# Five row blocks of a graph layer from gathered rows, and weights asked for one at a time

## The chip, the cores and the metric

The kernel runs on one core of a Trainium2 chip. The core has a matrix engine (TensorE, PE in the profile, with PEld for its weight loads), a vector engine (VectorE, DVE), a scalar engine (ScalarE, ACT), a general engine (GpSimd, POOL), and DMA queues that SyncE (SP), ACT and POOL issue from. Each engine works through its instructions in the order in which the program gives them. The metric is the time of one execution on the device in microseconds, as the median of several runs. The kernel before takes 1496.76 us, median of 3 runs (1496.23 to 1499.8).

## The reference

There are N = 2708 nodes with D = 256 features, and a matrix adj in which about 0.3% of the entries and the diagonal are nonzero. Two layers follow one another. Layer 0 is the part that the change is in:

```python
support = adj @ x
support = jnp.concatenate([x, support], axis=1)
x = _layernorm(x + relu(support @ weight + bias))
```

Layer 1 takes R = (adj + I), each row divided by its sum, and twice over does Xf = R @ Xf and Xa = A @ Xa, where A is a softmax attention over all nodes of which each row keeps the fewest largest entries that hold 0.9 of its mass. Each step adds Xf @ U1.T + Xa @ U2.T to Z. Two layer norms end it.

## The kernel before, in words

The nodes are cut into NB = 22 row blocks of P = 128 (the last has 20 rows, and is called EDGE). In DRAM adj is kept by blocks: `adj_d[m, :, k, :]` is the transposed 128 x 128 tile of row block m and column block k, and one DMA of a half row block brings 11 such tiles (704 KB). All arithmetic is float32. The order of the work is written out by hand: the program's order on each engine and on each DMA queue is the order on the chip, and semaphores order the engines among each other.

**Start.** adj @ x @ w0[D:] is computed as adj @ y0 with y0 = x @ w0[D:], so y0 comes first: 22 row blocks (line 385), whose copies out of PSUM alternate between ACT (line 388, odd blocks) and DVE (line 390, even ones). SP's queue loads xT in seven pieces (line 194), then adj of block 0. ACT's queue asks for all weights ahead of its first copy: both halves of w0 (line 188), then b0, w1, w3, w2, the four matrices u1 and u2, and the two rows gb (lines 198 to 206). y0 has one more column of ones, so that the row sums of adj come out of the same product.

**Layer 0's loop** runs over the row blocks m in their order, 0 to 21. In each:

- `name_columns(m)` on DVE finds for each of the 128 partitions which of the 22 tiles holds a nonzero, and writes the name of each such row of adj_d as a number (lines 282 to 288; the diagonal tile is left out). It reads the same halves of adj that PE multiplies.
- `adj_product` on PE multiplies 22 tiles by y0 into a PSUM tile acc, of which there are two (line 250; EDGE has a form of its own at line 247, in four column groups that `edge_sum` adds, and needs its acc zeroed by DVE first).
- SP's queue loads the next block's two halves (line 220). There are three buffers of a half, so the second half waits until PE and DVE have both read the first half of the present block.
- PE adds xT times w0[:D] (line 452), then turns the x1 of the block before (`x1_transpose`, line 430), and after every fourth block `x1_qk` projects queries and keys for 512 columns (lines 415 to 422).
- DVE and ACT do bias, relu, residual and layer norm (lines 461 to 469), and SP stores x1 (lines 467 and 470).

**Lists.** Class `Lists` makes from the names of a group of row blocks the lists of rows to gather. `turn` transposes the names on PE; `take` extracts the eight largest names of each row with a MAX8 and a MATCH_REPLACE8 on DVE (lines 314 and 315), 20 times for a list of 160; `end` packs the pieces through DRAM: a store and a load on POOL's queue (lines 327 and 328), a scan on DVE that waits for them (line 332), seven indirect scatters (line 338), and a load of the list into `ix` (line 341). The groups are blocks 0 to 15, whose list is taken during the last six blocks of layer 0 and ended behind them, and blocks 16 to 21, whose list is made during step 1 of layer 1.

**Layer 1** starts with `begin1` (logits, line 496, and the u1 projections, line 621). It uses the lists: `adj_gather` brings up to 896 rows of adj_d per row block with CC = 7 indirect DMAs of 128 rows on POOL's queue (line 360), so R @ Xf takes 8 products instead of 22. The rows of the other factor are gathered in the same way (line 670). Four large tiles es[0] to es[3] hold the attention rows in layer 1; in layer 0 they hold w0 (es[0]), b0 and w1n (es[1]), and the names and the first list's room (es[3]). The lines that hold the loop's order around a block are

```python
        adj_product(acc, m, y0, D + 1, False)
        if m == EDGE:
            acc = edge_sum(acc, D + 1, False)
        if m + 1 < NB:
            adj_load(m + 1, 0)
            adj_load(m + 1, 1)
```

## Time and profile before

| what | value |
| --- | --- |
| median of 3 runs | 1496.76 us (1496.23 to 1499.8) |
| the profiled execution | 1397.94 us |
| its span, first to last instruction | 1396.1 us |
| mean granted TensorE clock in it | 0.957 |
| PE busy in the span | 1287.6 us (92%) |
| DVE busy | 1054.3 us (76%) |
| ACT busy | 757.1 us (54%) |
| POOL busy | 645.5 us (46%) |
| DMA | 157.95 MB, mean 113 GB/s |

The profile is one execution, and that one was 98.8 us shorter than the median of the runs. Its page gives busy times, the span in 40 slices of 34.9 us each, the groups of instructions by line, and the waits. In a line of the timeline the first number is the start in us, the second the length in us, then come the engine (a q behind it means its queue), the line of the kernel, the operation, what is written and read, the shape, and how many were merged; in brackets stand the idle time before it and what ended that. A float32 matmul shows as two MATMUL instructions. In a line of the windows the columns are the stretch, its length, the busy time of PE, PEld, DVE, ACT and POOL with the number of instructions, the granted clock, the share of the DMA engines' time and GB/s.

### The profile page before, as it was taken

The page shows a single profiled execution, that of the slowest core. Times are in us where ns is not written, and L with a number is a line of the kernel's source. Part 1 is how long each engine was busy: PE and PEld are TensorE (multiplying, and loading weights), DVE is VectorE, ACT ScalarE, POOL GpSimd, SP SyncE. Part 2 cuts the span into 40 slices and gives each one's busy share as a digit, 9 for nine tenths or more (in the row PEclk, how much of TensorE's full clock was granted, in tenths as well). Part 3 has the DMA queues.
Part 4 walks back from the last instruction along what each step waited for, and adds up shares of the span by engine and source line. Part 5 has one row for each costly group of instructions (what it writes and reads, how often), then busy time and mean ns, then how long its engine had stood idle before and what let it go on. Part 6 is the DMA issues. An engine that isn't in the chain of part 4 may idle for free.

```text
span 1396.1 us, 19129 instructions
## 1 busy us (share of the span) xinstructions
PE 1287.6 (92%) x5788; PEld 903.6 (65%) x5788; DVE 1054.3 (76%) x3624; ACT 757.1 (54%) x1381; POOL 645.5 (46%) x595
## 2 busy tenths in 40 slices
PE   5999999989899999999999869999998998999885
PEld 4778778743466666766676447676765665666662
DVE  1445445784988887777771399999999999999995
ACT  1100000015455555555554468887878989998942
POOL 1000000004374431776555287877726557777771
PEclk8999999999999999999999889999999999999986
DMA  7345445422222210232223255464523434544441
GB/s 211 102 147 161 144 157 159 138 83 68 76 74 76 64 62 9 73 93 79 66 65 100 76 162 162 140 182 132 157 62 117 130 117 140 162 138 127 140 129 45
DMA packets 92831, 157.95 MB, mean 113 GB/s; under 512 B 16356, under 2 KB 65196, under 8 KB 92720
## 3 DMA queue, kind: packets, MB, share of 16 engines
q1 hardware_dynamic: 66434, 100.59, 22.2%
q0 software_dynamic: 20544, 51.17, 13.4%
q10 hardware_dynamic: 5742, 4.89, 1.3%
q8 instruction: 48, 0.79, 0.2%
q14 instruction: 63, 0.52, 0.1%
HBM read 125.33 MB, written 31.26 MB: 112 GB/s over the span
## 4 chain that ended last, share of the span: by engine, by line
PE 54%; DVE 38%; ACT 2%; DMA 2%; issue 2%; SPq 0%; ACTq 0%; DVEq 0%
PE acc L536 16%; PE acc L250 15%; PE lg L496 6%; DVE cand L950 6%; DVE w L981 5%; DVE e L984 5%; DVE w L947 4%; PE tr L516 4%; PE misc L649 3%; DVE spare L551 3%; DVE srt L549 3%; PE acc L621 2%; PE misc L420 2%; PE acc L452 2%; PE misc L415 2%
## 5 line engine op out<-in xcount | busy, mean ns | idle before, releaser
L536 PE MATMUL acc<-ya,wT 128*128 128x256 f32 (+1 forms) x924 | 241.2, 402 | 2.8 <-ACT wT L519 2.8
L519 ACT COPY wT<-tr 128x512 f32<-128x512 f32 (+2 forms) x264 | 133.7, 510 | 201.3 <-PE tr L516 198.4
L670 POOL DMA_INDIRECT yg<-yf_d,ix x154 | 196.6, 1276 | 80.6 <-PE misc L702 43.7
L536 PE MATMUL acc<-x,wT 128*128 128x256 f32 (+1 forms) x924 | 230.5, 388 | 0.0
L536 PEld LDWEIGHTS acc<-x,wT 128*128 128x128 f32 (+1 forms) x924 | 165.2, 189 | 79.6 <-issue 46.9
L536 PEld LDWEIGHTS acc<-ya,wT 128*128 128x128 f32 (+1 forms) x924 | 177.8, 199 | 58.0 <-issue 25.7
L250 PE MATMUL acc<-y,adj_t 128*128 128x257 f32 (+1 forms) x924 | 208.8, 382 | 0.0
L670 POOL DMA_INDIRECT yg<-v_d,ix x154 | 169.8, 1103 | 77.6 <-DMA v_d<-v 32.4
L250 PEld LDWEIGHTS acc<-y,adj_t 128*128 128x128 f32 (+1 forms) x924 | 171.5, 189 | 34.0 <-issue 10.3
L360 POOL DMA_INDIRECT adj_t<-in_adj,ix x154 | 169.3, 1099 | 50.9 <-issue 39.6
L496 PE MATMUL lg<-k,q 64*128 64x512 f32 (+3 forms) x528 | 155.3, 617 | 35.3 <-ACT e L794 33.4
L702 PE MATMUL misc<-yg,adj_t 128*128 128x256 f32 (+1 forms) x660 | 175.1, 397 | 12.8 <-DVE v L725 5.2
L516 PE MATMUL tr<-ident,e 128*128 128x128 f32 (+1 forms) x968 | 153.1, 278 | 16.8 <-DVE bulk L985 14.2
L516 PEld LDWEIGHTS tr<-ident,e 128*128 128x128 f32 (+1 forms) x968 | 117.4, 142 | 64.3 <-issue 30.2
L702 PEld LDWEIGHTS misc<-yg,adj_t 128*128 128x128 f32 (+1 forms) x660 | 117.4, 192 | 62.0 <-issue 18.2
L327 POOL DMA_DIRECT2D part_d<-e x1 | 0.6, 573 | 307.5 <-DVE e L326 307.5
L542 DVE MAX8 cand<-e 128x8 f32<-128x170 f32 (+1 forms) x352 | 88.1, 319 | 39.9 <-ACT e L503 39.9
L894 ACT ACTIVATE w<-e,st 128x2708 f32<-128x2708 f32 (+1 forms) x43 | 113.5, 2640 | 0.0
L431 ACT COPY x1T<-tr 128x256 f32<-128x256 f32 (+1 forms) x22 | 8.0, 364 | 192.1 <-PE tr L430 192.1
L897 ACT ACTIVATE w<-e,st 128x2708 f32<-128x2708 f32 (+1 forms) x42 | 111.0, 2642 | 0.1
L950 DVE MAX8 cand<-w 128x8 f32<-128x136 f32 (+1 forms) x440 | 94.4, 285 | 0.8
L549 DVE MAX8 srt<-spare 128x8 f32<-128x128 f32 (+3 forms) x264 | 81.4, 308 | 9.1
(227 smaller groups left out, 1849.4 us busy)
## 6 DMA issues: line engine op xcount, KB each, us to landing
adj_t<-in_adj SPq DMA_DIRECT2D x44, 704.0 KB
adj_t<-adjc_d SPq DMA_DIRECT2D x44, 448.0 KB
adjc_d<-adj_t SPq DMA_DIRECT2D x22, 256.0 KB
base<-za_d SPq DMA_DIRECT2D x41, 128.0 KB
adjc_d<-adj_t SPq DMA_DIRECT2D x22, 192.0 KB
xt<-in_x ACTq DMA_DIRECT2D x21, 128.0 KB
x_d<-x SPq DMA_DIRECT2D x21, 128.0 KB
x1b_d<-xb SPq DMA_DIRECT2D x21, 128.0 KB
```

The lines of the kernel that those rows point to most:

```text
L250: nc.tensor.matmul(acc[:p, :n], lhsT=halves[k // KH][:kw, k % KH, :p], rhs=y[:kw, k, :n], start=k == 0, stop=stop and k == NB - 1)
L360: nc.gpsimd.indirect_dma_start(out=a[:CW, i, :], out_offset=None, in_=adj_rows, in_offset=bass.IndirectOffsetOnAxis(ap=ix[:CW, m, i:i + 1] ...
L496: nc.tensor.matmul(lg[:p, h, :b - a], lhsT=q[o, t * P:t * P + p], rhs=keys[s][o, i, :b - a], start=True, stop=True)
L516: nc.tensor.transpose(tr[:kw, k % 4, :p], e[:p, k * P:k * P + kw], ident[:p, :p])
L519: nc.scalar.copy(wT[:, :full, :p], tr[:, :full, :p])
L536: nc.tensor.matmul(acc[:p, :D], lhsT=wT[:kw, k % 4, :p], rhs=y[:kw, k, :], start=k == 0, stop=k == NB - 1)
L549: nc.vector.max(dst[:p, i:i + 8], src[:p])
L670: nc.gpsimd.indirect_dma_start(out=y[:CW, i, :], out_offset=None, in_=rows_d, in_offset=bass.IndirectOffsetOnAxis(ap=ix[:CW, m, i:i + 1], ...
L702: nc.tensor.matmul(acc[:p, :D], lhsT=a[:kw, k, :p], rhs=rhs, start=k == 0, stop=k == CC)
L894: nc.scalar.activation(scr[:b.p, :N], e, AF.Relu, bias=b.nz, scale=b.l[k], accum_out=b.relu)
L897: nc.scalar.activation(scr[:b.p, :N], e, AF.Sign, bias=b.nz, scale=b.l[k], accum_out=b.sign)
L950: nc.vector.max(cand[:p, 8 * i:8 * i + 8], w[:p, SEG2 * i:SEG2 * (i + 1)])
```

## The change

The row blocks 16 to 20 are no longer multiplied tile by tile in layer 0. Their halves of adj are loaded into free parts of es[0] to es[2] during the first blocks, only to be named (`scan_load`, and a second `name_columns` in the same block); EDGE is brought forward to fourth place, and so the list of the group (16, 22) can be made early: it is turned in the seventh block of the order, taken 7 at a time in three blocks, and ended. y0 is stored to DRAM in the seventh block. Then `gather0` brings the listed rows of adj_d and of y0 with seven indirect DMAs each, and `sparse_product` makes the product from 8 matmuls. The five gathered blocks alternate with the dense blocks 12 to 15 behind block 11; there is room for two at a time. The other two lists are (0, 12), taken during the last blocks, and (12, 16), taken in step 1 of layer 1 where the second list was.

Of the weights, ACT's queue asks for w0[D:] only at first; the others follow one at a time, six between its y0 copies and five in the first blocks of the loop.

```diff
--- before.py
+++ after.py
@@ -37,7 +37,10 @@
 TIE_EPS = 1.5e-5
 KS = 7
 CAP = 160
-ML = 16
+GROUPS = ((16, 22), (0, 12), (12, 16))
+SPARSE = (16, 17, 18, 19, 20)
+
+ORDER = (0, 1, 2, 21, 3, 4, 5, 6, 7, 8, 9, 10, 11, 16, 12, 17, 13, 18, 14, 19, 15, 20)
 CW, CC = 128, 7
 
 
...
@@ -184,9 +189,11 @@
     w0 = es[0][:, :2 * DC * D].rearrange("p (c e) -> p c e", e=D)
     b0 = es[1][:, :D]
     w1n = es[1][:DA, D:2 * D].rearrange("a (c p) -> a c p", p=P)
-    for h in (1, 0):
+    def w0_load(h):
         nc.scalar.dma_start(out=w0[:, h * DC:(h + 1) * DC, :],
                             in_=w0_d[h * D:(h + 1) * D].rearrange("(c p) e -> p c e", p=P))
+
+    w0_load(1)
 
     xT = big.tile([P, DC, N], FP, tag="Y", name="xT")
     xT_v = xT_d.rearrange("(c p) n -> p c n", p=P)
...
@@ -195,15 +202,18 @@
 
     make_identity(nc, ident)
     nc.gpsimd.memset(c.eps, LN_EPS)
-    nc.scalar.dma_start(out=b0, in_=b0_d[None, :].to_broadcast([P, D]))
-    nc.scalar.dma_start(out=c.w1, in_=w1_d.rearrange("(c p) a -> p c a", p=P))
-    nc.scalar.dma_start(out=c.w3, in_=w3_d.rearrange("(c p) a -> p c a", p=P))
-    nc.scalar.dma_start(out=c.w2, in_=w2_d)
-    for s in range(2):
-        nc.scalar.dma_start(out=c.u1[:, :, s, :], in_=u1_d[s].rearrange("(c p) e -> p c e", p=P))
-        nc.scalar.dma_start(out=c.u2[:, :, s, :], in_=u2_d[s].rearrange("(c p) e -> p c e", p=P))
-    nc.scalar.dma_start(out=c.gb[:, 0, :], in_=g_d[None, :].to_broadcast([P, D]))
-    nc.scalar.dma_start(out=c.gb[:, 1, :], in_=b_d[None, :].to_broadcast([P, D]))
+
+    weights = [lambda: w0_load(0),
+               lambda: nc.scalar.dma_start(out=b0, in_=b0_d[None, :].to_broadcast([P, D])),
+               lambda: nc.scalar.dma_start(out=c.w1, in_=w1_d.rearrange("(c p) a -> p c a", p=P)),
+               lambda: nc.scalar.dma_start(out=c.w2, in_=w2_d),
+               lambda: nc.scalar.dma_start(out=c.w3, in_=w3_d.rearrange("(c p) a -> p c a", p=P)),
+               lambda: nc.scalar.dma_start(out=c.gb[:, 1, :], in_=b_d[None, :].to_broadcast([P, D])),
+               lambda: nc.scalar.dma_start(out=c.gb[:, 0, :], in_=g_d[None, :].to_broadcast([P, D]))]
+    for u, u_d in ((c.u1, u1_d), (c.u2, u2_d)):
+        for s in range(2):
+            weights.append(lambda u=u, u_d=u_d, s=s: nc.scalar.dma_start(
+                out=u[:, :, s, :], in_=u_d[s].rearrange("(c p) e -> p c e", p=P)))
     nc.gpsimd.memset(flags, 0.0)
     fcol = small.tile([P, 1], FP, tag="fcol", name="fcol", bufs=1)
     onec = small.tile([P, 1], FP, tag="onec", name="onec", bufs=1)
...
@@ -263,23 +273,23 @@
...
-    def name_columns(m):
+    def name_columns(m, halves):
         for h in range(2):
-            nc.vector.tensor_reduce(some[:, h * KH:(h + 1) * KH], adj_of[m][h], AX.X, ALU.max,
+            nc.vector.tensor_reduce(some[:, h * KH:(h + 1) * KH], halves[h], AX.X, ALU.max,
...
@@ -386,6 +398,8 @@
                              start=j == 0, stop=j == DC - 1)
         if t % 2:
             nc.scalar.copy(y0[:p, t, :D], py[:p, :D])
+            if 3 <= t < 15:
+                weights.pop(0)()
         else:
             nc.vector.tensor_copy(y0[:p, t, :D], py[:p, :D])
 
...
@@ -434,29 +448,108 @@
         a, b = CHS[i]
         qk_project(0, a, b, lambda j: x1T[:, j, a:b])
 
+
+
+
+    scan_room = [r[:, a:a + KH * P].rearrange("p (k i) -> p k i", i=P)
+                 for r, a in ((es[2], 0), (es[0], 2 * DC * D), (es[1], 3 * D))]
+    gather_room = []
+    for (ry, ay), (ra_, aa), ao in (((es[2], 0), (es[0], 2 * DC * D), 0), ((es[1], 3 * D), (es[2], CC * (D + 1)), 1)):
+        ao = 2 * DC * D + CC * P + ao * P
+        gather_room.append((ry[:, ay:ay + CC * (D + 1)].rearrange("p (c d) -> p c d", d=D + 1),
+                            ra_[:, aa:aa + CC * P].rearrange("p (c i) -> p c i", i=P), es[0][:, ao:ao + P]))
+    to_scan, scanned, gathered = list(SPARSE), {}, {}
+    n_scans = 0
+
+    def scan_load():
+        nonlocal n_scans
+        m = to_scan.pop(0)
+        scanned[m] = []
+        for h in range(2):
+            a = scan_room[n_scans % 3]
+            n_scans += 1
+            nc.sync.dma_start(out=a, in_=adj_d[m, :, h * KH:(h + 1) * KH, :])
+            scanned[m].append(a)
+
+    y0_rows = c.y0_d.rearrange("p k d -> (p k) d")
+    to_gather = list(SPARSE)
+
+    def gather0():
+
+        if not to_gather:
+            return
+        m = to_gather.pop(0)
+        y, a, own = gather_room[SPARSE.index(m) % 2]
+        iy = small.tile([P, CC], I32, tag="iy", name="iy", bufs=2)
+        nc.sync.dma_start(out=own, in_=adj_d[m, :, m, :])
+        nc.gpsimd.tensor_scalar(iy[:CW], ix[:CW, m, :], m * P * NB, P * NB - 1, op0=ALU.subtract, op1=ALU.min)
+        for i in range(CC):
+            nc.gpsimd.indirect_dma_start(out=a[:CW, i, :], out_offset=None, in_=adj_rows,
+                                         in_offset=bass.IndirectOffsetOnAxis(ap=ix[:CW, m, i:i + 1], axis=0))
+        for i in range(CC):
+            nc.gpsimd.indirect_dma_start(out=y[:CW, i, :], out_offset=None, in_=y0_rows,
+                                         in_offset=bass.IndirectOffsetOnAxis(ap=iy[:CW, i:i + 1], axis=0))
+        gathered[m] = y, a, own
+
+    def sparse_product(acc, m, y0):
+        y, a, own = gathered.pop(m)
+        for i in range(CC):
+            nc.tensor.matmul(acc[:, :D + 1], lhsT=a[:CW, i, :], rhs=y[:CW, i, :], start=i == 0, stop=False)
+        nc.tensor.matmul(acc[:, :D + 1], lhsT=own, rhs=y0[:, m, :], start=False, stop=False)
+
     CB = CH // P
-    lists = Lists(0, ML, flags[:, NF - 4:NF - 2], first_room)
-    for m in range(NB):
+    TURN = len(SPARSE) + 1
+    dense = [m for m in ORDER if m not in SPARSE]
+    done, n_qk = set(), 0
+
+    def x1_done(m):
+
+        nonlocal n_qk
+        x1_transpose(m)
+        done.add(m)
+        while n_qk < len(CHS) and all(k in done for k in range(CB * n_qk, min(NB, CB * n_qk + CB))):
+            x1_qk(n_qk)
+            n_qk += 1
+
+    lists = Lists(0, first_room)
+    taken = 0
+    scan_load()
+    for i, m in enumerate(ORDER):
         p = rows(m)
         xt = work.tile([P, D], FP, tag="in", name="xt", bufs=3)
         nc.scalar.dma_start(out=xt[:p], in_=x_d[m * P:m * P + p, :])
+        if weights and i:
+            weights.pop(0)()
         acc = edge_acc if m == EDGE else ps_acc()
-        name_columns(m)
-        adj_product(acc, m, y0, D + 1, False)
-        if m == EDGE:
-            acc = edge_sum(acc, D + 1, False)
-        if m + 1 < NB:
-            adj_load(m + 1, 0)
-            adj_load(m + 1, 1)
+        if m in SPARSE:
+            sparse_product(acc, m, y0)
+            gather0()
+        else:
+            name_columns(m, adj_of[m])
+            if scanned and m != EDGE:
+                name_columns(*scanned.popitem())
+            adj_product(acc, m, y0, D + 1, False)
+            if m == EDGE:
+                acc = edge_sum(acc, D + 1, False)
+            dense.pop(0)
+            if dense:
+                adj_load(dense[0], 0)
+                adj_load(dense[0], 1)
+            if to_scan and m != EDGE:
+                scan_load()
+            elif i == len(SPARSE) + 1:
+                for a, b in ((0, KH), (KH, NB - 1)):
+                    nc.sync.dma_start(out=c.y0_d[:, a:b, :], in_=y0[:, a:b, :])
+                nc.sync.dma_start(out=c.y0_d[:rows(NB - 1), NB - 1, :], in_=y0[:rows(NB - 1), NB - 1, :])
         for j in range(DC):
             nc.tensor.matmul(acc[:p, :D], lhsT=xT[:, j, m * P:m * P + p], rhs=w0[:, j, :],
                              start=False, stop=j == DC - 1)
-        if m:
-            x1_transpose(m - 1)
-        if m == ML:
+        if i:
+            x1_done(ORDER[i - 1])
+        if i in (TURN, ORDER.index(GROUPS[1][1] - 1) + 1):
+            if i > TURN:
+                lists, taken = Lists(1, first_room), 0
             lists.turn()
-        if m >= CB and m % CB == 0:
-            x1_qk(m // CB - 1)
         h = work.tile([P, D], FP, tag="mid", name="h")
         nc.vector.tensor_add(h[:p], acc[:p, :D], b0[:p])
         nc.vector.scalar_tensor_tensor(h[:p], h[:p], 0.0, xt[:p], op0=ALU.max, op1=ALU.add)
...
@@ -468,20 +561,26 @@
         xb = work.tile([P, D], FP, tag="x1b", name="xb")
         nc.vector.tensor_add(xb[:p], x1[:p, m, :], c.gb[:p, 1, :])
         nc.sync.dma_start(out=c.x1b_d[m * P:m * P + p, :], in_=xb[:p])
-        if m == EDGE - 1:
+        if ORDER[i + 1:i + 2] == (EDGE,):
             edge_acc = ps_acc(EDGE)
-        if m >= ML:
-            i = m - ML
-            lists.take(CAP // 8 * i // (NB - ML), CAP // 8 * (i + 1) // (NB - ML))
+        if i >= TURN and taken < CAP // 8:
+            n = 7 if lists.i == 0 else 3
+            lists.take(taken, min(CAP // 8, taken + n))
+            taken += n
+            if lists.i == 0 and taken >= CAP // 8:
+                lists.end()
+                gather0()
+                gather0()
+    assert not weights and not scanned and not gathered and taken >= CAP // 8
     lists.end()
     y_room = big.tile([P, DC * N], FP, tag="Y", name="yg")
     YW = 2 * (CC + 1) * D
     yg = y_room[:, :YW].rearrange("p (s c d) -> p s c d", s=2, d=D)
     spares = [y_room[:, YW + D * i:YW + D * (i + 1)] for i in range(4)]
-    lists = Lists(ML, NB, flags[:, NF - 2:], yg[:, 1].rearrange("p c d -> p (c d)"))
+    lists = Lists(2, yg[:, 1].rearrange("p c d -> p (c d)"))
     lists.turn()
-    x1_transpose(NB - 1)
-    x1_qk(len(CHS) - 1)
+    x1_done(ORDER[-1])
+    assert n_qk == len(CHS)
 
     NL = (len(CHS) + 1) // 2
 
```

More of the change, by code (lines that the diff above doesn't have):

```diff
@@ L82, in gnn_two_layer_kernel @@
     DC = D // P
+    assert sorted(ORDER) == list(range(NB)) and sorted(m for g in GROUPS for m in range(*g)) == list(range(NB))
     assert N % 2 == 0 and NB % 2 == 0 and N * 2.0 ** -15 < 0.09 and DC == 2 and DA == 64
@@ L102, in gnn_two_layer_kernel @@
     c.part_d = dram.tile([NB, KS, CAP + 1], FP, name="part_d")
-    c.list_ds = [dram.tile([b - a, KS * CAP], I32, name="list_d") for a, b in ((0, ML), (ML, NB))]
+    c.list_ds = [dram.tile([b - a, KS * CAP], I32, name="list_d") for a, b in GROUPS]
     c.adjc_d = dram.tile([NB, CW, CC * P], FP, name="adjc_d")
+    c.y0_d = dram.tile([P, NB, D + 1], FP, name="y0_d")
     c.yf_d = dram.tile([P, NB, D], FP, name="yf_d")
@@ L119, in gnn_two_layer_kernel @@
     c.rinv = const.tile([P, NB], FP, name="rinv")
-    NF = 6 * NB + 4
+    NF = 6 * NB + 2 * len(GROUPS)
     flags = const.tile([P, NF], FP, name="flags")
@@ L265, in fast_path @@
     first_room = room[:, at + 2 * NB:at + 2 * NB + LROOM]
-    zero = room[:P - rows(NB - 1), NW - D:]
+    zero = room[:P - rows(NB - 1), NW - D - 1:]
     nc.gpsimd.iota(ramp, pattern=[[-1, NB]], base=LAST, channel_multiplier=-NB,
@@ L269, in fast_path @@
     nc.gpsimd.memset(zero, 0.0)
-    for y_d in (c.yf_d, c.v_d):
-        nc.gpsimd.dma_start(out=y_d[rows(NB - 1):, NB - 1, :], in_=zero)
+    for y_d in (c.y0_d, c.yf_d, c.v_d):
+        nc.gpsimd.dma_start(out=y_d[rows(NB - 1):, NB - 1, :], in_=zero[:, :y_d.shape[2]])
     ix = small.tile([P, NB, CC], I32, tag="ix", name="ix", bufs=1)
     nc.gpsimd.iota(ix.rearrange("p m c -> p (m c)"), pattern=[[0, NB * CC]], base=LAST, channel_multiplier=0)
-    for i, (a, b) in enumerate(((0, ML), (ML, NB))):
+    for i, (a, b) in enumerate(GROUPS):
         nc.gpsimd.dma_start(out=c.list_ds[i][:, :CW * CC].rearrange("m (p c) -> p m c", c=CC), in_=ix[:, a:b, :])
@@ L290, in fast_path, with __init__ @@
     class Lists:
-        def __init__(self, a, b, flag, room):
-            self.a, self.b, self.n, self.flag = a, b, KS * (b - a), flag
+        def __init__(self, i, room):
+            self.i, (a, b) = i, GROUPS[i]
+            at = NF - 2 * len(GROUPS) + 2 * i
+            self.a, self.b, self.n, self.flag = a, b, KS * (b - a), flags[:, at:at + 2]
             at = 3 * P
@@ L334, in end @@
             nc.vector.scalar_tensor_tensor(to, run, before_m[:b - a], num, op0=ALU.add, op1=ALU.subtract)
-            list_d = c.list_ds[a > 0]
+            list_d = c.list_ds[self.i]
             flat = list_d.rearrange("m (s k) -> (m s) k", k=CAP)
@@ L374, in adj_store @@
         nc.sync.dma_start(out=c.own_d[m, :rows(m), :], in_=a[:rows(m), CC, :])
-    adj_load(0, 0)
-    adj_load(0, 1)
+    adj_load(ORDER[0], 0)
+    adj_load(ORDER[0], 1)
     y0 = big.tile([P, NB, D + 1], FP, tag="V", name="y0")
```

## The prediction

> **What bounds the kernel now.** I read the page's slices first, then the windows, then the timeline of layer 0 engine by engine. Layer 0 runs from the start to 309.8 us, where the first logits begin. In the busy tenths the first eight or nine slices are it:
>
> ```profile
> PE   5999999989899999999999869999998998999885
> DVE  1445445784988887777771399999999999999995
> POOL 1000000004374431776555287877726557777771
> ```
>
> TensorE (PE) is full after the first slice, VectorE (DVE) half busy, GpSimd (POOL) empty until slice 9. Two windows of the same stretch (PE, PEld, DVE, ACT, POOL busy, granted clock, DMA share, GB/s) say how much room the others have:
>
> ```profile
> 120.00:140.00 20.00, 20.00 (x93) 16.36 (x92) 11.48 (x25) 1.33 (x4) 0.00 (x0) 1.00 0.49 154
> 260.00:280.00 20.00, 20.00 (x92) 16.35 (x91) 18.11 (x41) 0.67 (x2) 0.00 (x0) 1.00 0.52 154
> ```
>
> So PE sets the pace, except at the start, where the timeline shows it idle 10.7 us for an ACT copy that stood behind ACT's own weight DMAs:
>
> ```profile
> 13.88 0.38 ACTq L204 DMA_DIRECT2D u<-in_u  x1
> ...
> 18.24 1.28 ACT L388 ACT_TABLE_LOAD   x1 [18.24 <-DMA u<-in_u]
> 19.53 0.37 ACT L388 COPY y<-misc 128x256 f32<-128x256 f32 x1
> ...
> 19.96 19.51 PE L385 MATMUL misc<-e,xT 128*128 128x256 f32 x76 [10.74 <-ACT y L388]
> ```
>
> A dense row block on PE, and beside it on DVE the naming of columns and (last three lines) one take of the list:
>
> ```profile
> 112.05 9.92 PE L250 MATMUL acc<-y,adj_t 128*128 128x257 f32 x44
> 114.94 3.14 DVE L282 TENSOR_REDUCE e<-adj_t 128x11 f32<-128x1408 f32 x2
> 121.90 1.13 PE L452 MATMUL acc<-e,xT 128*128 128x256 f32 x4
> ...
> 260.88 0.55 DVE L314 MAX8 e<-e 112x8 f32<-112x384 f32 x1
> 261.46 0.09 DVE L315 MATCH_VALUE_LOAD e<-e 112x8 f32 x1
> 261.54 0.54 DVE L315 MATCH_REPLACE8 e<-e 112x384 f32<-112x384 f32 x1
> ```
>
> The end of a list and the first gathers on POOL, which the change moves into layer 0:
>
> ```profile
> 314.25 0.57 POOL L327 DMA_DIRECT2D part_d<-e  x1 [307.54 <-DVE e L326]
> 319.95 0.93 POOL L338 DMA_INDIRECT list_d<-e,to  x1 [2.74 <-DVE to L334]
> 322.35 0.86 POOL L338 DMA_INDIRECT list_d<-e,to  x1 [1.47 <-DMA list_d<-e,to]
> 336.28 1.24 POOL L341 DMA_DIRECT2D ix<-list_d  x1 [1.40 <-DMA list_d<-e,to]
> 341.00 1.01 POOL L360 DMA_INDIRECT adj_t<-in_adj,ix  x1 [3.10 <-PE lg L496]
> 342.32 0.95 POOL L360 DMA_INDIRECT adj_t<-in_adj,ix  x1 [0.30 <-issue]
> ```
>
> Seven scatters, each waiting for the one before, then the list's load, then gathers 1.25 us apart.
>
> **What the Trainium skill says.** "GPSIMD Engine Reference", section Specifications: GpSimd shares its SBUF interfaces with VectorE and contends with instructions that have two SBUF inputs. The trace agrees: most gathers take 0.95 us, but one that starts at 823.86, beside a two-input DVE operation of 3.05 us, takes 2.72. "DMA: Bandwidth & Descriptors", section Issuing engines are not separate DMA queues: all queues share 16 engines; what was asked for later leaves them to xT. "TensorE: Matmul & The Clock Gate", section What's actually happening: an idle array is clocked at half. The trace: 0.50 from 12 to 24 us, 1.00 from 26.
>
> **The change, part by part.** A *start*. Ten of eleven weight requests leave ACT's queue ahead of its first copy. PE has three row blocks of y0 done by 9.2 us now. It would go on: one block at the unwarmed 1.7 us (copies at 22.07 and 23.78), 18 at 0.865 (ACT copies 1.73 apart, two blocks each), 15.6, and the 2.0 us from the last y0 product to the first block (39.47 to 41.45): 9.2 + 1.7 + 15.6 + 2.0 = 28.5 instead of 41.45, a gain of 13.0. xT with the rest is some 3.7 MB; the 2 us windows have moved that much by 18.5 us, when PE is at block 13 of 22, so it stays ahead. Warm from the first: 27.6; one xT chunk late: 32. The weights (0.4 us of ACT queue each) are needed only at block 0 or in layer 1.
>
> B *PE's work*. A dense block has a period of 11.03 (112.05 to 123.08): 22 products, 9.76, and 1.27 of xT products and transposes. A gathered block has 8 at 0.444 = 3.55, with the 1.27: 4.82. Five save 31.0. The edge block, now fourth, costs 10.6: 3.3 waiting for its zeroed PSUM behind the layer norm of the block before, and 7.3 as now. At the end the projections of two chunks (4.3 each) cover the last layer norm, for which PE now waits 2. PE alone: 16 x 11.03 + 5 x 4.82 + 5 x 4.3 + 10.6 + 3 = 235.7 against 268.4 now (41.45 to 309.83), a gain of 32.7.
>
> C *early scans*. Each adds 3.65 of DVE (3.14 + 0.18 + 0.25 and gaps) to 3.65 + 3.0 (layer norm, 112.03 to 115.0): 10.3, under the 11.03 of PE. Loads: 2.88 MB of adj a period and about 0.65 of x, stores and weights, 320 GB/s; the windows show 376 to 414 between 22 and 28 us. On SP's queue the scan loads stand behind the next block's loads and ahead of x1's stores; both fit. No cost, with 0.7 us of cover; if that is gone, five excesses. y0's store (2.9 MB, some 8 us of DMA) delays the loads behind it about to the end of their slack: 0 to 3, I take 0.
>
> D *takes*. A take is 1.245 (260.88 to 262.12). Let S6 be the start of the seventh block. Layer norm ends at S6 + 13.7. Then 7 takes 8.7, naming 3.65, norm 3.0, 7 takes 8.7, 3.65, 3.0, 6 takes 7.5, the end of the list 1.25: the list leaves DVE at S6 + 53. DVE then waits 5.1 for the list's way through DRAM (as at 319.08 now). Behind that stands the naming of the next block; behind that SP's load into the named buffer; behind that PE's second half. PE loses about 4 and 6 us in the tenth and eleventh blocks.
>
> E *gathers*. From the list's leaving DVE to the first gather: 27.0 for the first list now, 29.9 for the second (536.2 to 566.1, busy DMA). I take 30; ends 27 and 37. One block: 0.6 for the indices and 14 x 1.25 = 18.1; I add 0.9 for the two-input operations of layer norm: 19 (18 to 22). y0's rows of 1,028 bytes aren't in the trace; rows of 1,024 cost POOL the same 0.95. Each gather also puts the block's own rows (64 KB) on SP's queue, for two blocks ahead; no dense load stands behind it there. Five in a row, and 3 to land: the last block can begin at S6 + 53 + 30 + 95 + 3 = S6 + 181. PE by itself would be there at S6 + 150, with D's stalls at 159. So POOL's chain sets the end. The wait falls on the first gathered block (about 13) and a few us on later ones.
>
> *Sum*, in the profiled execution (span 1396.1, time 1397.94). S6 = 28.5 + 5 x 11.03 + 10.6 + 4.3 = 98.5; the last block starts at 279.5; 16 later (its 4.8, two chunks, the last transposes and projection) the logits: 295.5 against 309.8, **14 us earlier**. As gains and losses: 13.0 + 32.7 - 9 (D) - 22 (E). After that the order is as before: the second list leaves DVE some 7 us ahead of the logits instead of 4 behind them, so step 1's gathers wait for nothing new.
>
> The runs' median, 1496.76, is 98.8 above the profiled time, and no view says where. Spread evenly, the gain is 15. If TensorE is slower there (98.8 is 7.7% of its 1287.6), layer 0 grows by 21 now and by about 7 with the change, since takes and gathers don't slow: 28. I take 18: **1479 us**.
>
> **The rivals.** *Gathers in time* (1461): if the list came 20 us sooner than I sum it, only D's 9 would be lost, a gain of 36. For it: POOL is free. Against: the scatters' 2.24 us steps are plain. 0.15. *No difference* (1497): gathers 1.58 apart, the mean busy time of the yf rows in layer 1 (1276 ns) with 0.30 of issue. A block then costs POOL 22.7, five lose 18. For it: that mean. Against: the long ones there stand beside DVE operations of 3 us, of which layer 0 has none. 0.09. *Slower* (1513): POOL's price again, at 1.80, that row's busy and idle time together (196.6 + 80.6 over 154); a block costs 25.8, five lose 34. It decides from 1.63 on (5 x 4.5 us for 18 and the bound). For it: scans, dense loads and gathers share DMA; against: the 0.95 us is POOL's own work. 0.14. *It doesn't do what it says*: the start, if xT and not ACT holds PE; then 3 to 4 us less, inside the range.
>
> **How the numbers follow.** Main case 0.62, its own range 1467 to 1491 (gains 6 to 30: list 27 to 37, gather 18 to 22, clock). A measurement tells 0.3%, 4.5 us, from no change. Faster: 0.60 of the main case and 0.15: 0.75; same 0.02 + 0.09 = 0.11; slower 0.14. The range leaves out slower and a little of the fastest: 1460 to 1499.
>
> **What would show it.** First L250 product at 28 to 29 us instead of 41.45; period 11.0 through the scans; DVE without gaps for some 45 us from the seventh block; PE idle some 13 us ahead of the first gathered block, waiting for a gather; POOL unbroken for 95 us, gathers 1.25 apart; logits near 295. I am wrong if the gather pitch is over 1.5 us, if PE waits for loads during the scans, or if the first gathered block finds its rows there.

## The result, and the profile after

The changed kernel takes 1514.72 us, median of 4 runs (1513.89 to 1517.51), against 1498.08 us (1496.23 to 1499.8, 4 runs) for the kernel before: a ratio of 1.0115, 95% interval 1.0094 to 1.0135. It is slower by 16.6 us where 18 faster was forecast. Its profiled execution took 1513.99 us, with a span of 1512.1.

One thing has to be known to read all that follows: executions of these kernels come in two lengths, called the *longer* and the *shorter* below; the kernel before takes about 1498 us in every timed run beside the changed kernel above, and about 1399 in its profile and in all that was run later, so kernels are compared here within one length only. The changed kernel's profile in this section is of the longer length.

The page's slices of the changed kernel (a slice is 37.8 us), rows of TensorE, VectorE and GpSimd:

```profile
PE   7998957799899999999989499999878777777765
DVE  3669614745888878777712699999987777777776
POOL 1000275413554525765561776777254544455551
```

TensorE's first slice rose from 5 to 7, which is the start; GpSimd now works from the fifth slice on. But the sixth to eighth slices of TensorE read 5, 7 and 7 where it was full before, and in the last seven slices VectorE is at 7 where it was at 9, and TensorE lower too. The windows of the same trace (PE, PEld, DVE, ACT, POOL busy, granted clock, DMA share, GB/s) show the hole:

```profile
120.00:140.00 20.00, 19.08 (x87) 15.27 (x86) 18.78 (x48) 1.04 (x3) 0.00 (x0) 1.00 0.35 120
200.00:220.00 20.00, 9.61 (x22) 5.41 (x22) 1.54 (x6) 0.00 (x0) 15.38 (x17) 0.59 0.33 87
220.00:240.00 20.00, 12.74 (x38) 7.07 (x39) 0.00 (x0) 0.96 (x2) 15.11 (x17) 0.76 0.30 78
```

Between 200 and 240 us only GpSimd is busy as planned; DMA is at a third. The timeline of the changed kernel: the start, one of the gathers of y0, and then the hole, engine by engine:

```profile
8.38 9.76 PE L397 MATMUL misc<-e,xT 128*128 128x256 f32 x44 [0.46 <-ACT y L400]
...
19.34 1.99 PE L397 MATMUL misc<-e,xT 128*128 128x256 f32 x8 [1.20 <-ACT y L400]
...
22.76 6.82 PE L397 MATMUL misc<-e,xT 128*128 128x256 f32 x28 [1.43 <-ACT y L400]
...
31.57 1.79 PE L260 MATMUL acc<-y,adj_t 128*128 128x257 f32 x7
...
203.62 0.95 POOL L490 DMA_INDIRECT e<-y_d,iy  x1 [0.30 <-issue]
...
209.42 0.38 PE L444 MATMUL tr<-ident,x 128*128 128x128 f32 x2
...
221.77 0.37 ACT L445 COPY x1T<-tr 128x256 f32<-128x256 f32 x1 [25.57 <-issue]
222.20 3.78 PE L429 MATMUL misc<-x1T,wqq 128*128 128x512 f32 x4 [12.40 <-issue]
...
231.57 0.58 ACT L435 COPY q<-misc 128x512 f32<-128x512 f32 x1 [9.43 <-remote]
...
236.46 0.59 PE L260 MATMUL acc<-y,adj_t 128*128 128x257 f32 x1 [2.69 <-issue]
...
238.59 0.59 PE L260 MATMUL acc<-y,adj_t 128*128 128x257 f32 x1 [1.54 <-issue]
...
329.56 2.08 PE L595 MATMUL lg<-k,q 64*128 64x512 f32 x4
```

The start is as forecast to 3 us, the gathers take 0.95 us of GpSimd and stand 1.25 apart, also for y0's rows of 1,028 bytes. The transposes end at 209.8, and ScalarE's copy of them, which waits for nothing else, begins 12 us later. Then TensorE idles 1.5 to 2.7 us ahead of single products, with nothing named that they wait for. Such a product takes 0.59 us, where the median of all products is 0.38; but by far most of the time is lost in late starts. The logits, the last line, start at 329.56, where the prediction had 295.5. In the profile before, the same line is

```profile
309.83 2.08 PE L496 MATMUL lg<-k,q 64*128 64x512 f32 x4
```

### The profile page after: what moved, and what is told of

The parts are those of the page before. It is cut to its first block, busy times and chain, and to the rows that moved or that the text cites. A ratio compares the mean times of both kernels' runs of the same rounds, so it can differ in the third digit from the quotient of the medians.

```text
span 1512.1 us, 19095 instructions
## 1 busy us (share of the span) xinstructions
PE 1286.5 (85%) x5651; PEld 888.7 (59%) x5651; DVE 1081.1 (71%) x3692; ACT 756.5 (50%) x1382; POOL 699.4 (46%) x682
## 4 chain that ended last, share of the span: by engine, by line
PE 44%; DVE 30%; ACT 10%; issue 6%; another core or an unknown queue 4%; DMA 3%; POOL 1%; ACTq 0%; SPq 0%; POOLq 0%; DVEq 0%
PE acc L635 15%; PE acc L260 7%; PE lg L595 5%; PE tr L615 4%; DVE cand L1049 4%; DVE w L1080 4%; DVE w L1046 3%; PE misc L748 3%; DVE e L1083 3%; DVE spare L650 2%; DVE srt L648 2%; PE acc L720 2%; DMA adj_t<-in_adj 2%; ACT w L996 2%
## 5 line engine op out<-in xcount | busy, mean ns | idle before, releaser
L635 PE MATMUL acc<-ya,wT 128*128 128x256 f32 (+1 forms) x924 | 247.6, 410 | 63.6 <-ACT wT L618 45.0
L635 PEld LDWEIGHTS acc<-ya,wT 128*128 128x128 f32 (+1 forms) x924 | 181.2, 204 | 119.9 <-ACT wT L618 49.7
L769 POOL DMA_INDIRECT yg<-yf_d,ix x154 | 193.1, 1254 | 104.2 <-PE misc L801 42.0
L801 PE MATMUL misc<-yg,adj_t 128*128 128x256 f32 (+1 forms) x660 | 179.9, 402 | 21.9 <-issue 12.0
L769 POOL DMA_INDIRECT yg<-v_d,ix x154 | 147.5, 958 | 86.9 <-issue 41.4
L260 PE MATMUL acc<-y,adj_t 128*128 128x257 f32 x704 | 166.6, 392 | 16.2 <-issue 9.5
L260 PEld LDWEIGHTS acc<-y,adj_t 128*128 128x128 f32 x704 | 134.0, 194 | 45.5 <-issue 18.5
```

Of the source, the lines that this page charges most:

```text
L260: nc.tensor.matmul(acc[:p, :n], lhsT=halves[k // KH][:kw, k % KH, :p], rhs=y[:kw, k, :n], start=k == 0, stop=stop and k == NB - 1)
L635: nc.tensor.matmul(acc[:p, :D], lhsT=wT[:kw, k % 4, :p], rhs=y[:kw, k, :], start=k == 0, stop=k == NB - 1)
L769: nc.gpsimd.indirect_dma_start(out=y[:CW, i, :], out_offset=None, in_=rows_d, in_offset=bass.IndirectOffsetOnAxis(ap=ix[:CW, m, i:i + 1], ...
L801: nc.tensor.matmul(acc[:p, :D], lhsT=a[:kw, k, :p], rhs=rhs, start=k == 0, stop=k == CC)
```

## The experiments

The expectations name theories by letters and say what each holds. What I came to hold after the first two sets, and called theory L and theory P from there on, is that the prediction's working of layer 0 holds in the shorter execution (P, GpSimd's chain sets its end), and that the longer one adds lateness beside GpSimd's gathers (L).

**The kernel before again.** No edit. It was to show where the 98.8 us between profile and runs lie.

> The kernel before, unchanged, once more. Theory S (signals between engines come late while rows of 1 KB are gathered on POOL's queue, in whatever kernel): an execution near 1497 us, with layer 0, which has no gathers, as before (logits at 310 us, within 1) and the 100 us beyond the profiled 1396 in step 2 of layer 1, beside the gathers of yf and v, as gaps of PE and ACT that no wait explains. Theory D (the executions are disturbed as a whole): the excess is spread over all stages, layer 0 too, about 7% in each, so logits at 330.

1397.19 us, logits at 310.7. Both theories missed, because the execution was a shorter one again; nothing was told apart.

**Loads in place of gathers.** The changed kernel, with the rows of adj, of y0, or of both fetched for the five blocks by plain loads on SyncE's queue (always the first seven row blocks' worth, so the five blocks are not what layer 0 asks for):

```diff
-        for i in range(CC):
-            nc.gpsimd.indirect_dma_start(out=a[:CW, i, :], out_offset=None, in_=adj_rows,
-                                         in_offset=bass.IndirectOffsetOnAxis(ap=ix[:CW, m, i:i + 1], axis=0))
+        nc.sync.dma_start(out=a[:CW], in_=adj_d[m, :, :CC, :])
-        for i in range(CC):
-            nc.gpsimd.indirect_dma_start(out=y[:CW, i, :], out_offset=None, in_=y0_rows,
-                                         in_offset=bass.IndirectOffsetOnAxis(ap=iy[:CW, i:i + 1], axis=0))
+        nc.sync.dma_start(out=y[:CW], in_=c.y0_d[:, :CC, :])
```

Both changed:

> The changed kernel, but the rows of adj and of y0 for the five blocks come by two plain DMAs on SP's queue (the first 7 tiles of the block and the first 7 blocks of y0, so those five row blocks of the result are not what the layer asks for). Theory S: POOL's chain and the gaps both go; PE's own order holds: logits at S6 + 159 + 16, near 275 us. Theory D: the gaps of 200 to 250 us stay in part, logits at 300 or later.

6581 us: what layer 0 then computes makes layer 1's lists overflow, and the general path behind the tuned one ran as well. Only its layer 0 can be read: logits at 285.9, where 275 was expected. The first product came at 33.9 us, not 28.5, and TensorE lost some 14 us, not 9, to the waits for loads behind the takes. Only y0's rows loaded:

> The changed kernel, but only the y0 rows come by a plain DMA on SP's queue (the first 7 blocks of y0, so five row blocks are not what the layer asks for); the rows of adj are still gathered by POOL, 7 gathers a block, some 9 us. Theory S in its narrow form (only the rows of 1 KB do it): no gaps; first gathered block at about 200 us, logits near 280. In its wide form (any gather): gaps of half the length remain, logits near 300. Theory D: as changed, near 325.

1372.95 us, logits at 282.5, where the kernel before took 1400.26. Only adj's rows loaded:

> The changed kernel, but only the rows of adj come by a plain DMA on SP's queue (the first 7 tiles of the block, so five row blocks are not what the layer asks for); the y0 rows are still gathered by POOL. Theory S in its narrow form (rows of 1 KB): gaps as in the changed kernel, 30 us in all, logits at 310 or later. In its wide form: half of that, near 295. Theory D: near 325.

1371.17 us, logits at 282.9. The two whose time can be read were shorter ones, and none had a hole, so they say nothing on it. What they do say is that halving GpSimd's work for the five blocks, either half, brings layer 0's end 12 us forward of the changed kernel's 294.25 (next run): in the shorter execution GpSimd's chain sets that end, as step E had it.

**The change again, and its start alone.** The changed kernel as it is:

> The changed kernel, unchanged, on the same chip as the kernel before, which there takes some 1400 us rather than 1497. Theory S (a property of the kernel's y0 gathers): logits again at 325 to 330, and the kernel slower than before by some 15 us. Theory E (the executions come in two kinds, one of about 1400 and one of about 1500 us for the kernel before; only the second holds signals back beside gathers): the first kind here, no gap behind the first gathered block, logits at 296 as the prediction's sum has it, and a time near 1384, that is 14 to 16 us less than before.

The kernel before with only the weights asked for late, one at a time (`w0_load(1)` first, the other eleven from the list `weights`):

> The kernel before with the start of the change alone: weights asked for later and one at a time. First dense product at 31.6 us as in the changed kernel, instead of 41.5; all later stages shifted by 10 us. Both theories: about 10 us less than before. If the later stages give it back (the u weights arriving during the loop), less than 5.

| kernel | us (range) | ratio to before, 95% | first product | logits |
|---|---|---|---|---|
| before | 1399.46 (1395.19 to 1401.23) | | 41.7 | 310.7 |
| changed, again | 1382.71 (1378.41 to 1386.49) | 0.9884 (0.9850 to 0.9918) | 31.4 | 294.25 |
| start alone | 1386.44 (1382.86 to 1390.17) | 0.9920 (0.9894 to 0.9947) | 29.0 | 296.9 |

The kernel before's first product and logits are from the trace of its first repeat above. In the shorter execution the change gains 16.7 us. The start alone gains 13.0 of it, 3 more than was expected of it, since its first product comes at 29.0 and not at 31.6:

```profile
29.03 10.02 PE L254 MATMUL acc<-y,adj_t 128*128 128x257 f32 x44
```

The five gathered blocks bring only some 4 more, although they take some 31 us of work from TensorE (the prediction's sum): GpSimd's chain and the waits for takes eat the rest, as the runs below bear out. The windows and the timeline of this shorter execution of the changed kernel, against the longer one above:

```profile
200.00:220.00 20.00, 18.95 (x59) 11.69 (x60) 5.97 (x19) 2.17 (x5) 15.09 (x18) 0.80 0.45 125
220.00:240.00 20.00, 20.00 (x92) 16.26 (x92) 16.90 (x43) 1.33 (x4) 15.31 (x17) 1.00 0.66 207
```

```profile
200.02 1.20 PE L497 MATMUL acc<-e,e 128*128 128x257 f32 x2 [3.77 <-DMA e<-y_d,iy]
...
209.36 0.38 PE L444 MATMUL tr<-ident,x 128*128 128x128 f32 x2
...
209.78 0.37 ACT L445 COPY x1T<-tr 128x256 f32<-128x256 f32 x1 [11.82 <-PE tr L444]
...
210.20 1.98 PE L429 MATMUL misc<-x1T,wqq 128*128 128x512 f32 x4 [0.46 <-ACT x1T L445]
...
212.22 0.58 ACT L435 COPY q<-misc 128x512 f32<-128x512 f32 x1 [2.07 <-PE misc L429]
...
279.69 0.70 PE L497 MATMUL acc<-e,e 128*128 128x257 f32 x2 [0.86 <-DMA e<-y_d,iy]
...
294.25 2.08 PE L595 MATMUL lg<-k,q 64*128 64x512 f32 x4
```

The first and the last gathered block (200.02 and 279.69) wait for a gather of y0's rows, so GpSimd's chain still holds TensorE at the end of the five. The transposes begin at 209.4 in both; ScalarE's copy follows 0.4 us later here and 12.4 us later there. Matching every instruction of TensorE, VectorE and ScalarE in the two traces by line and order gives how far the longer execution is behind (my own table from the two traces, medians of 20 us windows; the scatters of the lists are not counted as gathers):

| stretch of the shorter execution, us | behind at its end, us | grown by | gathers issued in it |
|---|---|---|---|
| 0 to 200 | -1.8 | -1.8 | 10 |
| 200 to 280 | 37.3 | 39.1 | 28 of adj, 32 of y0 |
| 280 to 360 | 35.1 | -2.2 | 10 of adj |
| 360 to 740 | 41.8 | 6.7 | 144 of adj, 7 of yf |
| 740 to 820 | 60.5 | 18.7 | 34 of yf or v |
| 820 to 1060 | 61.6 | 1.1 | 126 of yf or v |
| 1060 to 1340 | 132.7 | 71.1 | 136 of yf or v |
| 1340 to the end | 131.4 | -1.3 | none |

All the lateness comes after GpSimd's first gather (187.0 us in the longer trace, 187.7 in the shorter), and nearly all beside gathers of rows of y0, yf or v, though not beside all of them. The seven scatters of the first list, from 160 to 181 us, came without any. A slower TensorE is not it: from 360 to 740 us, where TensorE is busy for 377.5 of 380 us in the shorter execution, only 6.7 us are added. Nor are slower or fuller DMA transfers: between 200 and 245 us a packet of gathered rows of y0 takes 0.24 us on average in both traces, and the DMA engines are less busy in the longer one (shares of 0.33 and 0.30 against 0.45 and 0.66).

Layer 0's share is 35 us (329.56 - 294.25), that of layer 1 is 131.4 - 35.3 = 96.1. The kernel before has no gather in layer 0 and is longer by 1498.08 - 1399.46 = 98.6 in all, nearly what the changed kernel is in layer 1 alone. Theory L asks for that; where the kernel before loses its 98.6 no trace shows. The result on record is then -16.7 + 131.4 - 98.6 = +16.1, where +16.6 was measured; that sum closes wherever in the kernels the lateness lies, so it is no evidence for the place.

**Gathers alone, and four blocks.** First the kernel before once more, for a trace of its longer execution:

> The kernel before, unchanged, for its trace. Executions of it have taken either about 1399 us or about 1498. Theory L (in the longer kind other engines' instructions come late while GpSimd's gathers are under way, and only then): if this one is of the longer kind, the first logits begin at 309 to 313, since its layer 0 has no gather, and the whole excess of some 98 us lies behind them. Theory U (the longer kind is slower evenly, or wherever TensorE works, as the prediction had it): 330. If it is of the shorter kind: 1399, logits at 310, and nothing is told apart.

1398.78 us (19 runs), logits at 311.35: a shorter one, nothing told apart. Then the start alone with 70 gathers in layer 0 that nobody reads, so that nothing waits for a list or a row:

```diff
+    def extra_gathers(m):
+        nc.gpsimd.tensor_tensor(extra_y[:, 0, :], x1[:, m, :], x1[:, m, :], op=ALU.add)
+        ...  (7 gathers of rows of adj, 7 of rows of x)
+        if m in (6, 8, 10, 12, 14):
+            extra_gathers(m - 1)
```

> The late weights alone, and beside layer 0's seventh to fifteenth row blocks 70 gathers on GpSimd that nobody reads: five times 7 of 128 rows of adj (512 bytes each) and 7 of 128 rows of x (1,024 bytes), each five started behind a layer norm. The output is what it was. The start alone took 1386.4 where the kernel before took 1399. Theory L: in the shorter kind the same 1386 within 4, logits at 297; in the longer kind 20 to 35 us above the start alone, so 1505 to 1520, with gaps on TensorE and ScalarE beside the gathers and logits at 317 to 332. Theory C (gathers cost VectorE and TensorE a shared port or bandwidth whatever the kind): over 1392 in the shorter kind too. Theory N (the gathers alone are harmless, and it is the waits of the gathered blocks that cost): 1386 or 1485, logits at 297 in both kinds.

1385.86 us (1385.25 to 1390.03), logits at 297.9, beside 1386.44 and 296.9 without them. The gathers were at the same pitch of 1.25 us. In a shorter execution 70 gathers beside dense blocks cost nothing; theory C falls. The Trainium skill ("GPSIMD Engine Reference", section Specifications) has GpSimd contend with VectorE's two-input operations for the SBUF interfaces that they share; in layer 0 this costs no more than the 0.1 to 0.2 us by which at most two gathers in fourteen are longer (1.05 to 1.18 against 0.95).

Then four gathered blocks instead of five:

```diff
-SPARSE = (16, 17, 18, 19, 20)
+SPARSE = (17, 18, 19, 20)
-ORDER = (0, 1, 2, 21, 3, 4, 5, 6, 7, 8, 9, 10, 11, 16, 12, 17, 13, 18, 14, 19, 15, 20)
+ORDER = (0, 1, 2, 21, 16, 3, 4, 5, 6, 7, 8, 9, 10, 11, 17, 12, 18, 13, 19, 14, 20, 15)
```

> The change with four gathered blocks instead of five; row block 16 is taken densely as the fifth. Theory P (in the shorter kind GpSimd's chain of list and gathers sets the end of layer 0 with five, TensorE with four): start of the list one dense block earlier, S5 = 87; GpSimd's last block ready at S5 + 53 + 30 + 4 x 19 + 3 = 249; TensorE by itself there at 28.5 + 4 x 11.03 + 10.6 + 12 x 11.03 + 9 + 3 x 4.8 = 239 to 249; logits 281 to 286 against 294.3 with five, the time about 1371 to 1375. Rival Q (TensorE's saved products are lost to VectorE's takes and waits, not to GpSimd): one fewer gathered block costs 6 us, logits at 300, 1389. Theory L for the longer kind: 14 gathers fewer in layer 0, so about 7 us less lost there, 1493 to 1503.

1376.76 us (1375.93 to 1379.79), ratio 0.9853 (0.9831 to 0.9875): four gathered blocks are 6 us *faster* than five. Layer 0's end explains a part of the 6: the logits come at 291.8, against 294.25 here and 292.6 in the next run of the changed kernel; the rest lies in layer 1 or in the spread of the runs. Its timeline:

```profile
144.76 0.16 DVE L344 TENSOR_TENSOR_SCAN run<-e 6x7 f32<-6x7 f32 x1 [4.57 <-DMA e<-part_d]
...
150.97 7.40 PE L260 MATMUL acc<-y,adj_t 128*128 128x257 f32 x22 [8.15 <-DMA adj_t<-in_adj]
...
208.13 3.21 PE L497 MATMUL acc<-e,e 128*128 128x257 f32 x14
```

The first gathered block (208.13) waits for nothing any more, so TensorE sets the pace again, as theory P says (the list also starts one block earlier, with the first gather at 174.0 instead of 187.7); rival Q, with logits at 300, is out. But they were at 291.8, not 281 to 286: the first product came at 32.2, not 28.5, and the waits for loads behind VectorE's takes (the 8.15 and the stretched product after it) came to 11 us, not 9.

**The change a third time, and its gathers alone.**

> The changed kernel once more, for its kind. In executions where the kernel before takes about 1399 it took 1382.7, in those where it takes about 1498 it took 1514.7. Theory L (in the longer kind instructions come late beside GpSimd's gathers): 1383 within 5 or 1515 within 5, never between, with the kernel before beside it at 1399 or 1498. Theory U (a slowdown of any size, spread over engines): times between.

1384.12 us (1379.06 to 1384.31), ratio 0.9892 (0.9858 to 0.9925), logits at 292.6: shorter, and a gain of 13.9 us over the 1398.03 of the kernel before beside it. The changed kernel with the weights asked for at the head of ScalarE's queue, as before:

> The change without its late weights: the weights are asked for at the head of ScalarE's queue, as in the kernel before, and the five gathered blocks stay. Theory P (GpSimd's chain sets the end of layer 0, and it hangs on when the first six blocks are done): the whole of layer 0 is as late as its first product, 13 us, so logits at 307 against 310.7 of the kernel before, and 1395 to 1397 where that takes 1399, a gain of 2 to 4. Rival A (the gathered blocks bring more without the start, since scans and weights don't meet): logits under 300, 1388. In the longer kind Theory L expects 1527 to 1531.

1395.96 us (1390.15 to 1400.05, 12 runs), ratio 0.998 (0.9964 to 0.9997), logits at 309.8. The gain of 2 us is within what theory P gave, 2 to 4, and far from rival A's; the logits came 3 us later than its 307. With the start's 13.0 it makes 15.1, where the whole gave 16.7 and 13.9: the parts add up within the spread of the runs.

**VectorE's waits taken away.** Four blocks, five takes a block, and the end of the list cut where it waits for DRAM: VectorE names the next block's columns in between.

```diff
             nc.gpsimd.dma_start(out=self.all, in_=c.part_d[a:b])
+
+        def place(self):
+            a, b = self.a, self.b
             run = small.tile([NB, KS], FP, tag="run", name="run", bufs=1)[:b - a]
...
             name_columns(m, adj_of[m])
+            if to_place:
+                to_place.pop().place()
+                gather0()
+                gather0()
...
-            n = 7 if lists.i == 0 else 3
+            n = 5 if lists.i == 0 else 3
...
                 lists.end()
-                gather0()
-                gather0()
+                to_place.append(lists)
```

> Four gathered blocks, and the list in five takes a block instead of seven, its end cut in two: VectorE names the next block's columns while the counts are on their way through DRAM, and only then works out where the parts go. With four blocks alone TensorE waited some 11 us for loads behind VectorE's takes (5.2 - 5.0, 8.15, 7.4 - 5.0 and less), and the gathers were there 13 to 16 us ahead of need. Theory P (those waits, the prediction's step D, are now what is left on TensorE's path): list leaves VectorE some 7 us later, the wait of 5.1 is filled, VectorE is at most 8 us behind instead of 17, TensorE loses 1 to 4 us instead of 11, logits at 282 to 286 against 291.8, and the time 1367 to 1371 against 1376.8. Rival G (the later list brings GpSimd's chain back to the end): first gathered product waits for a gather, logits at 291 or later, 1376 to 1382.

This kernel left out the second half of the third list, so that in layer 1 row blocks 12 to 15 gathered one row over and over; its 1382.74 us say nothing. Its layer 0 can be read: logits at 284.4, in theory P's 282 to 286. With that list completed, and beside it the kernel before for its longer execution:

> The kernel before once more, for a trace of one of its longer executions (about 1498 us), which no look has caught yet. If this is one: Theory L (instructions of the other engines come late while GpSimd's gathers are under way, and only then) says first logits at 309 to 313, all of the excess of about 98 us in layer 1, durations of single instructions unchanged, and gaps of 1 to 3 us in front of short instructions beside the gathers. Theory U (TensorE slower, or all of it evenly) says logits at 330. If it is a shorter one: 1399 and logits at 311.

> The four gathered blocks with five takes a block and the end of the list cut in two, now with the third list's second half as well, which the one before left out (its row blocks 12 to 15 in layer 1 gathered a single row). That one had its first logits at 284.4 where four blocks alone had 291.8. Theory P (what layer 0 gains comes through to the end as it did with four blocks): logits 284 to 285, 1376.8 - 7 = 1370, range 1367 to 1373, where the kernel before takes 1399. Rival W (layer 1 waits anyway for the second list, whose end is set by VectorE): 1376 to 1383 as measured without the third list. In the longer kind Theory L expects 56 gathers in layer 0 instead of 70, so 0.8 of the 35 us lost there: 1370 + 98 + 28 = 1496.

The kernel before took 1398.95 us (10 runs), shorter. The completed version took 1370.95 us (1369.87 to 1371.69), ratio 0.9796 (0.9778 to 0.9814), logits at 284.8: theory P to the microsecond. Of the 7 us gained in layer 0, 5.8 come through to the end. Fewer takes a block and the cut end were changed together, so the shares of the two are not known. In its timeline the scan of the counts waits 2.32 instead of 4.57, and TensorE's longest wait for a load is 1.05 instead of 8.15:

```profile
147.89 5.02 PE L260 MATMUL acc<-y,adj_t 128*128 128x257 f32 x22 [0.55 <-DMA adj_t<-in_adj]
...
153.96 5.24 PE L260 MATMUL acc<-y,adj_t 128*128 128x257 f32 x22 [1.05 <-DMA adj_t<-in_adj]
154.15 0.16 DVE L347 TENSOR_TENSOR_SCAN run<-e 6x7 f32<-6x7 f32 x1 [2.32 <-DMA e<-part_d]
```

In shorter executions this version is 28 us faster than the kernel before and 12 faster than the change. How it does in a longer one wasn't seen.

**For a longer execution, twice more.** The kernel before and the kernel with only adj's rows gathered (its five blocks again not what layer 0 asks):

> The kernel before, for a trace of one of its longer executions. Theory L: in one of about 1498 us, logits at 309 to 313, the records of semaphores thin out from the first scatter of the first list on (about 320 us, where the changed kernel's trace on record has them thin out from 160 us), and the excess lies beside the gathers that follow. Theory U: logits at 330, records thin from the start. In one of 1399: logits at 311, nothing told apart.

> The change with the rows of y0 loaded plainly (its first seven row blocks, in one load on SyncE's queue) and only the rows of adj gathered, so that the five blocks aren't what layer 0 asks; it took 1373 where the kernel before takes 1399, with logits at 282.5. Against the changed kernel's trace on record 28 us of the 35 us came beside the first two blocks' gathers of y0. Theory L with the y0 rows as its seat: in an execution of the longer kind logits still at 282 to 288. Theory L with any gather: 300 to 320. In a shorter one 1373 again.

1396.71 us, and 1366.29 us with logits at 281.8. And the kernel before with the kernel of the extra gathers:

> The last look for an execution of the kernel before at about 1498 us. Theory L: logits at 309 to 313 and the whole excess beside layer 1's gathers; Theory U: logits at 330. At 1399 and logits at 311 nothing is told apart.

> The late weights and 70 gathers in layer 0 that nobody reads, beside it: 1386 in a shorter execution, as measured. In a longer one Theory L expects 1505 to 1520 with logits at 317 to 332, Theory N 1485 with logits at 297.

1400.54 us, and 1390.42 us. All four were shorter ones. No experiment met a longer execution, so the lateness was never switched on or off on purpose.

## Why the prediction was wrong

**A, the start: right.** 13.0 us were forecast; alone it brings 13.0, with its first product at 29.0 where 28.5 was worked out. (The list of weights has twelve requests, of which eleven move; the prediction counted one fewer of each.) In the change TensorE waits another 2.6 us for the ScalarE copies of y0 (1.20 and 1.43 in the first lines of the timeline), so the first product comes at 31.4 to 31.6. These two copies stand behind weight requests in ScalarE's own queue, and the view puts the waits down to loads of xT and adj still on their way:

```profile
18.34 0.53 ACTq L209 DMA_DIRECT2D w<-in_w  x1
18.92 0.37 ACT L400 COPY y<-misc 128x256 f32<-128x256 f32 x1 [2.95 <-DMA xT<-in_xT]
21.92 0.37 ACTq L210 DMA_DIRECT2D w<-in_w  x1
22.34 0.37 ACT L400 COPY y<-misc 128x256 f32<-128x256 f32 x1 [3.05 <-DMA adj_t<-in_adj]
```

The "32" named for one chunk of xT late has the number, but not quite the cause: a load of xT is in it only by way of a weight request, and the second wait ends with a load of adj.

**B and C: right.** The seventh block begins at 101.77 (98.5 forecast, the 3 us of A), and the dense blocks before it keep their period through the early scans (42.51 to 53.54 in the third run of the change: 11.03).

**D, the takes: right, and worth more attention than it got.** The list leaves VectorE at S6 + 52.9 (53 forecast). TensorE loses 1.2, 5.5 and 3.0 us in the blocks beside and behind the takes in the third run of the change, 9.7 (9 forecast; 10.4 and 12.4 in its other two traces). I booked this as a price; it was a choice, and the last version took nearly all of it back.

**E, the gathers on GpSimd: right in size.** First gather 32 to 33 us after the list (30), a gathered block 18.0 us (19), pitch 1.25. GpSimd's chain does set layer 0's end with five blocks and not with four. In the shorter execution, which is the one whose profile was costed, the sum was 14 us earlier and 1397.94 - 14 = 1383.9; measured were 15.6 on the logits of the two traces (309.83 - 294.25) and 1382.71 us. Some of that closeness is luck: the start and the first gather came 3 us late each, and the five blocks of gathers made up for it by taking some 5 us less than summed.

**The step that failed is the one after the sum:** "The runs' median, 1496.76, is 98.8 above the profiled time, and no view says where. Spread evenly, the gain is 15. If TensorE is slower there [...] I take 18." For the changed kernel its own two traces refute both ways of spreading: the first 200 us are not longer at all (-1.8 us), the 380 us in which TensorE is fullest are longer by 6.7, and TensorE's busy time grew by 23 us of the 131 (1286.5 against 1263.4). The excess sits mostly in late starts after the first gather, 35 us of it in the stretch to which the change moved 70 gathers. So the term that I made +4 (14 to 18) was about -33: a gain of 16.7 us in the shorter execution and a loss of 16.6 in the longer one. None of the rivals had it: *slower* at 1513 gave the right time by chance, with gathers 1.80 apart, and they are 1.25 apart.

The three signs that were to prove me wrong did not appear: the pitch held, TensorE kept its period during the scans, and the first gathered block did wait for a gather, though 5.42 us ahead of it (3.77 in the shorter trace) and some more between its products, not 13. The numbers of layer 0 were right to a few us until 209 us and the result still fell on the other side, because 98.8 us that I could not place were given a place by assumption. With that much unexplained, a rival was due in which the excess follows what the change adds.

**What stays open.** That the gathers *cause* the lateness is argued, not shown: for it are that it begins some 20 us after the first of them, that it is absent up to there, and that the changed kernel's lateness in layer 1 (96.1 us) is near all that the kernel before has (98.6). Against it, or at least not explained: 126 gathers between 820 and 1060 us, 113 of them of yf, came with 1 us of lateness, 136 of v after them with 71. A rival that nothing here rules out: the trace's own records of semaphores become fewer from the first gather on as well (last section), so lateness and gathers, or lateness and recording, may have a cause in common. A trace of the kernel before at 1498 us would show whether its layer 0 is undisturbed, and none was met. What puts an execution into one length or the other is unknown.

## What to carry to other kernels

Where the profiled execution and the timed runs differ by more than the effect sought, the difference is the first thing to place; until then a rival should let it grow with exactly what the change adds. When work moves from a full engine to an empty one, work out the new engine's whole chain first: with five gathered blocks GpSimd's chain set the end, and four were no slower, though TensorE had more to do. A wait on the way through DRAM in a busy engine's order held up here what was queued behind it; splitting the step there, putting the next block's work between and taking fewer pieces a block, all three at once, took TensorE's waits for loads from 11 us to under 2.

## What the runs showed of the hardware

- One and the same changed kernel took 1382.7 and 1514.7 us. The durations of its instructions agree between the two traces by their medians (gather 952 ns in both, product 379 ns in both); the starts do not.
- The records of semaphore updates in the two traces are equal in number up to 180 us, 2,054 in the longer and 2,053 in the shorter, with the scatters of the first list among them, and fall apart from the first gather (187 us) on: 9,750 against 19,653 for the rest, nine tenths of the difference on semaphores that DMAs raise. Whether updates came late and together or only their records are missing, the traces don't say; where they are missing, the releasers named in the waits of the longer trace ("remote", "issue") are not to be relied on.
- A gather of 128 rows by an indirect DMA occupies GpSimd for 0.95 us at a pitch of 1.25 (medians), whether the rows have 512, 1,024 or 1,028 bytes, and 70 of them beside full dense blocks left the time of a shorter execution as it was.
